# Graph attention on one core: the product q[src] x q[dst] reads q[dst] from PSUM, and the one-hot products are made one block ahead

## The chip, the cores and the metric

The kernel runs on one core of one Trainium2 chip. A core has five engines that run side by side, each with its own queue of instructions: TensorE (PE; its weight loads are listed apart as PEld), VectorE (DVE), ScalarE (ACT), GpSimd (POOL) and SyncE (SP). They wait for each other on semaphores. TensorE writes its results to PSUM, of which there are eight banks; everything else lies in SBUF or in DRAM and is moved by DMA. POOL issues the indirect DMAs (gathers by index), SP all the others of the main loop.

The metric is the time of one execution in microseconds on the device. Nine executions of the kernel before took 3247.66 to 3299.46 us, with a median of 3289.91 us.

## The reference

One layer of a graph network with 12500 nodes and 212500 edges, sorted by dst. All features have 128 elements, 8 heads of 16.

```
h = relu(layernorm(x))
q, v = h @ Wq.T + bq, h @ Wv.T + bv          # per node
k = edge_attr @ Wk.T + bk                    # per edge
in_m   = sum(q[src] * k,      per head)      # three logits per edge and head
out_m  = sum(q[dst] * k,      per head)
diag_m = sum(q[src] * q[dst], per head)
score = (softmax of each, over the edges of one dst; summed) * edge_weight ** lam
h2 = segment_sum(score * v[dst], dst)
out = x + leaky_relu(h2 @ Wo.T + bo, 0.1)
```

The segment softmax has a maximum, an exponential and two sums over the edges of each node. As the edges are sorted, all of these are scans along the edges.

## The kernel before

The path for sorted edges (`ordered_path`) has three parts. A preparation computes q for all nodes and writes it to DRAM twice: `q_table`, in float32, and `q3_table`, as three bfloat16 terms whose sum is q. The main loop goes over the edges. A last part adds up per node and applies Wo.

The main loop works on blocks of 512 edges (128 partitions x JN = 4). The edges are cut into S = 5 stretches, and a step t takes one block of each stretch, s = 0 to 4: T = 84 steps, 420 blocks, and block number g = 5 t + s. For one block:

- `gather` (L608): POOL issues four indirect DMAs, which fetch q[src] from `q_table` into half 0 of the tile qq. It is called LOOK = 9 blocks ahead; there are QQ = 11 qq tiles. A gather waits until the last reader of its tile is done.
- `fetch_edges` (L600): SP loads the edge features ea, 6 blocks ahead into 7 tiles.
- `turn` (L940, L942): TensorE transposes ea into eT_ps, ScalarE copies it to eT.
- `project` (L948, L950): TensorE makes k in k_ps (two banks), the bias first.
- `spread_q` (L959, L961): because edges are sorted by dst, the q[dst] of a block lie within a window of 42 nodes. SP has loaded this window of `q3_table` (the tile win, L926, two tiles with five loads for each step t). Four matmuls of a one-hot matrix (oh) with win put q[dst] into qd_ps, for which there is one bank. ScalarE copies it into half 1 of qq.
- `one_hots` (L934, L935): ScalarE makes the one-hots of the next step from a list of relative indices (relb, loaded by SP, L916).
- `logits` (L968, L969, L971): VectorE multiplies half 0 and half 1 of qq (L968), both halves by k (L969), and sums over 16 elements for each head (L971).

Once per step t, and each at a given s, the scans follow: `turn_logits` and `turn_sums` at s = 0 (L984, L991, L1049, L1050), `scan_max` at s = 1 (L1001, L1004), `to_rows` (the matmuls of w_ps, L1062, and the copy L1067) and `powers` (L1012 to L1019) at s = 2, `scan_sums` (L1025, L1029) and the fetches for step t + 2 (L916, L920, L926) at s = 3, `select` (L1038) and `put_rows` (SP writes the sums, L1074) at s = 4.

The order of the work is written out by hand. `pin` ties each instruction to the one that was pinned before it on the same engine, so each engine, SP's and POOL's queues among them, runs its instructions in the order in which the loop calls them. The loop calls, for each g: gather, fetch_edges, project(g + 1), turn(g + 2), spread_q(g + 2), logits(g), one_hots, and then what s asks for. Where a tile is used again, the waits follow from its last readers.

PSUM is full: two banks each of eT_ps and k_ps, one of qd_ps, three that the small tiles of the scans share.

Of the kernel before, what the change touches and what calls it, by code (L numbers as in the profile page):

```python
# [472 lines left out]
def ordered_path(ctx: ExitStack, tc: tile.TileContext, flag, x, src, dst, edge_attr, edge_weight,  # L473
# [17 lines left out]
    nc = tc.nc  # L491
# [83 lines left out]
    def pin(inst):  # L575

        engine = str(inst.ins.engine)
        if engine in pinned:
            tc.add_manual_dep(inst.ins, pinned[engine], mybir.DependencyInfo(
                mybir.DependencyClass.NoSync, mybir.DependencyReason.DATA), reason="in order")  # L580
        pinned[engine] = inst.ins.name
        return inst
# [8 lines left out]
    qqs, st, eas = {}, {}, {}  # L591

    def fetch_edges(g):
        if g < S * T:
            ea = load.tile([P, JN * F], F32, name="ea", bufs=EA)
            b0 = (g % S * G + g // S) * BE
            n = min(BE, E - b0)
            if n < BE:
                nc.vector.memset(ea, 0.0)
            pin(nc.sync.dma_start(ea[:n // JN, :],  # L600
                                  edge_attr[b0:b0 + n, :].rearrange("(p j) f -> p (j f)", j=JN)))
            eas[g] = ea

    def gather(g):
        if g < S * T:
            qq = gath.tile([P, JN, 2, F], F32, name="qq")
            for j in range(JN):
                pin(nc.gpsimd.indirect_dma_start(  # L608
                    out=qq[:, j, 0, :], out_offset=None, in_=q_table,
                    in_offset=bass.IndirectOffsetOnAxis(  # L610
                        ap=src_i[:, g % S * G + g // S, j:j + 1], axis=0)))
            qqs[g] = qq
# [287 lines left out]
    with tc.tile_pool(name="work", bufs=2) as work, \  # L900
            tc.tile_pool(name="scan", bufs=2) as scan, \
            tc.tile_pool(name="ps", bufs=1, space=PSUM) as ps:
        ks, eTs, lTs, base_v = {}, {}, {}, {}
        end = S * T

        def block_rows(t):
# [3 lines left out]
        def fetch(t):  # L910

            if t >= T:
                return
            at, part = block_rows(t)
            relb = load.tile([K3, S, BE], BF, name="relb")
            pin(nc.sync.dma_start(relb, rel_d[part].rearrange("(s b) e -> s b e", b=G)  # L916
                                  [None, :, at, :].to_broadcast([K3, S, BE])))
            fa = load.tile([4 * S, BE], BF, name="fa", bufs=4)
            for s in range(S):
                pin(nc.sync.dma_start(fa[4 * s:4 * s + 4], fa_d[s * G + t]))  # L920
            _, base_v[t] = nc.values_load_multi_w_load_instructions(
                bases[0:1, t, 0:S], engines=[mybir.EngineType.SP], min_val=0, max_val=N - 1,
                skip_runtime_bounds_check_because="the indices of nodes are below N")
            win = load.tile([K3, S, F], BF, name="win")
            for s in range(S):
                pin(nc.sync.dma_start(win[:, s, :], q3_table[bass.ds(base_v[t][s] * 3, K3), :]))  # L926
            st[t] = dict(relb=relb, fa=fa, win=win)

        def one_hots(t, s):

            if s == 0:
                st[t]["oh"] = work.tile([K3, S, BE], BF, name="oh")
            d = st[t]["relb"][:, s, :]
            pin(nc.scalar.activation(d, d, AF.Abs, bias=before[:K3]))  # L934
            pin(nc.scalar.activation(st[t]["oh"][:, s, :], d, AF.Relu, bias=1.0, scale=-1.0))  # L935

        def turn(g):
            eT_ps = ps.tile([P, JN, P], F32, name="eT_ps", bufs=2)
            for j in range(JN):
                pin(nc.tensor.transpose(eT_ps[:, j, :], eas[g][:, j * F:(j + 1) * F], ident))  # L940
            eT = work.tile([P, JN, P], F32, name="eT", bufs=3)
            pin(nc.scalar.copy(eT, eT_ps))  # L942
            eTs[g] = eT
            del eas[g]

        def project(g):
            k_ps = ps.tile([P, JN, F], F32, name="k_ps", bufs=2)
            pin(nc.tensor.matmul(k_ps, ones3, bk3, start=True, stop=False))  # L948
            for j in range(JN):
                pin(nc.tensor.matmul(k_ps[:, j, :], eTs[g][:, j, :], wk, start=False,  # L950
                                     stop=(j == JN - 1)))
            ks[g] = k_ps
            del eTs[g]

        def spread_q(g):
            s, d = g % S, st[g // S]
            qd_ps = ps.tile([P, JN, F], F32, name="qd_ps")
            for j in range(JN):
                pin(nc.tensor.matmul(qd_ps[:, j, :], d["oh"][:, s, j * P:(j + 1) * P],  # L959
                                     d["win"][:, s, :], start=(j == 0), stop=(j == JN - 1)))  # L960
            pin(nc.scalar.copy(qqs[g][:, :, 1, :], qd_ps))  # L961

        def logits(g):
            s, t = g % S, g // S
            if s == 0:
                lTs[t] = scan.tile([P, JN, S, H3], F32, name="lT")
            prod = work.tile([P, JN, 3, F], F32, name="prod")
            pin(nc.vector.tensor_mul(prod[:, :, 2, :], qqs[g][:, :, 0, :], qqs[g][:, :, 1, :]))  # L968
            pin(nc.vector.tensor_mul(prod[:, :, 0:2, :], qqs[g],  # L969
                                     ks[g][:, :, None, :].to_broadcast([P, JN, 2, F])))  # L970
            pin(nc.vector.tensor_reduce(lTs[t][:, :, s, :],  # L971
                                        prod.rearrange("p j i (h d) -> p j (i h) d", d=DIM), AX.X,
                                        ALU.add))
            del ks[g], qqs[g]

        last = {}

# [100 lines left out]
        def later(f, t):  # L1078
            if 0 <= t < T:
                f(t)  # L1080
# [5 lines left out]
        turn(0)  # L1086
        turn(1)
        spread_q(0)
        spread_q(1)
        project(0)  # L1090
        for g in range(end + 2 * S):
            s, t = g % S, g // S
            if g < end:
                gather(g + LOOK)
                fetch_edges(g + AHEAD)
            if g + 1 < end:
                project(g + 1)
            if g + 2 < end:
                turn(g + 2)
                spread_q(g + 2)  # L1100
            if g < end:
                logits(g)
            if t + 1 < T:
                one_hots(t + 1, s)
            if s == 0:
                later(turn_logits, t - 1)
                later(turn_sums, t - 2)
            elif s == 1:
                later(scan_max, t - 1)
            elif s == 2:  # L1110
                later(to_rows, t - 2)
                later(powers, t - 1)
            elif s == 3:
                later(scan_sums, t - 1)
                if t + 2 < T:
                    fetch(t + 2)
            else:
                later(select, t - 1)
                later(put_rows, t - 2)
# [67 lines left out]
@with_exitstack  # L1187
def kernel(ctx: ExitStack, tc: tile.TileContext, x, src, dst, edge_attr,
                              edge_weight, Wq, bq, Wk, bk, Wv, bv, Wo, bo, lam, out):

    nc = tc.nc
    given = (x, src, dst, edge_attr, edge_weight, Wq, bq, Wk, bk, Wv, bv, Wo, bo, lam, out)
    flags = ctx.enter_context(tc.tile_pool(name="flags", bufs=1))
    flag = flags.tile([1, 1], I32, name="flag")
    ordered_path(tc, flag, *given)
    other = nc.values_load(flag[0:1, 0:1], min_val=0, max_val=1)
    with tc.If(other != 0):
        general_path(tc, *given)  # L1200
# [29 lines left out]
```

## Time and profile before

| | |
|---|---|
| nine executions | 3247.66 to 3299.46 us, median 3289.91 |
| the profiled execution | 3280.52 us, of which the span of its instructions is 3278.7 us |
| granted TensorE clock, mean | 0.727 |
| busy: PE, PEld | 1787.5 us (55%), 1440.6 us (44%) |
| busy: DVE, ACT, POOL | 2140.5 us (65%), 1521.7 us (46%), 1739.4 us (53%) |
| DMA | 345.21 MB, mean 105 GB/s |
| L608, gathers | 1680, 1706.4 us busy, mean 1016 ns, median 947 ns |
| L968, L969, L971 | 420 each, mean 680, 1215, 1753 ns |
| L959, L961 | 1680 with a mean of 261 ns, 420 with a mean of 590 ns |

No engine is busy for more than two thirds of the span. A line of the profile names the line of the kernel, the engine, the operation, what it writes and reads, and shapes; behind them stand the number of instructions, their busy time and the mean of one in ns, and then the idle time of the engine just before them with what ended most of it. "remote" means that a semaphore rose without an instruction in the trace that it can be put down to; "issue" means that the engine waited for nothing that the profile shows. In a timeline the first column is the start in us from the start of the span and the second the time in us; "x5" behind a line means that it stands for five instructions of the same kind, of which the first starts there. The ends of matmuls are modelled.

### The profile page before, as it was taken

The page shows a single profiled execution, that of the slowest core. Times are in us where ns is not written, and L with a number is a line of the kernel's source. Part 1 is how long each engine was busy: PE and PEld are TensorE (multiplying, and loading weights), DVE is VectorE, ACT ScalarE, POOL GpSimd, SP SyncE. Part 2 cuts the span into 40 slices and gives each one's busy share as a digit, 9 for nine tenths or more (in the row PEclk, how much of TensorE's full clock was granted, in tenths as well). Part 3 has the DMA queues.
Part 4 walks back from the last instruction along what each step waited for, and adds up shares of the span by engine and source line. Part 5 has one row for each costly group of instructions (what it writes and reads, how often), then busy time and mean ns, then how long its engine had stood idle before and what let it go on. Part 6 is the DMA issues. An engine that isn't in the chain of part 4 may idle for free. (4 is left out here: it accounts for less than half of the span.)

```text
span 3278.7 us, 35097 instructions
## 1 busy us (share of the span) xinstructions
PE 1787.5 (55%) x10635; PEld 1440.6 (44%) x10635; DVE 2140.5 (65%) x2178; ACT 1521.7 (46%) x2806; POOL 1739.4 (53%) x1714
## 2 busy tenths in 40 slices
PE   5245555555556545555545456555555546556567
PEld 4134444444444444444444344444444444445445
DVE  6556757667666667666667667566667666667754
ACT  5444445445454444444445444444445445445445
POOL 3545656646655556645656656555656555656100
PEclk8556767767776777777777767767767767767779
DMA  6643333333333333333333333333333333333152
GB/s 199 222 135 96 103 94 114 101 95 106 99 100 100 93 100 107 100 88 109 97 94 113 96 100 105 97 92 106 97 93 114 93 100 105 95 95 113 26 139 80
DMA packets 307123, 345.21 MB, mean 105 GB/s; under 512 B 134531, under 2 KB 225944, under 8 KB 306613
## 3 DMA queue, kind: packets, MB, share of 16 engines
q1 hardware_dynamic: 252474, 229.91, 23.6%
q0 software_dynamic: 54448, 112.96, 12.4%
q8 instruction: 85, 1.39, 0.2%
q14 instruction: 116, 0.95, 0.1%
HBM read 309.91 MB, written 32.76 MB: 105 GB/s over the span
## 5 line engine op out<-in xcount | busy, mean ns | idle before, releaser
L608 POOL DMA_INDIRECT qq<-q_table,src_i x1680 | 1706.4, 1016 | 1242.4 <-ACT qq L961 567.2
L950 PE MATMUL k_ps<-wk,eT 128*128 128x128 f32 x3360 | 658.0, 356 | 990.9 <-ACT eT L942 939.4
L950 PEld LDWEIGHTS k_ps<-wk,eT 128*128 128x128 f32 x3360 | 557.4, 251 | 1227.6 <-ACT eT L942 1044.3
L971 DVE TENSOR_REDUCE lT<-prod 128x96 f32<-128x1536 f32 x420 | 736.2, 1753 | 14.3
L1025 DVE TENSOR_TENSOR ew<-e,att_ps 120x512 f32<-120x512 f32 x84 | 57.8, 688 | 923.8 <-ACT e L1016 715.7
L942 ACT COPY eT<-eT_ps 128x512 f32<-128x512 f32 x420 | 246.2, 586 | 619.1 <-PE eT_ps L940 252.7
L969 DVE TENSOR_TENSOR prod<-qq,k_ps 128x1024 f32<-128x1024 f32 x420 | 510.4, 1215 | 26.7 <-remote 19.2
L1067 ACT COPY rows<-w_ps 126x288 f32<-126x288 f32 x84 | 33.6, 400 | 822.1 <-remote 783.9
L940 PE MATMUL eT_ps<-ident,ea 128*128 128x128 f32 x1680 | 344.2, 343 | 3.0 <-DVE found L881 2.9
L934 ACT ACTIVATE relb<-relb,before 126x512 bf16<-126x512 bf16 x420 | 307.7, 733 | 6.9 <-DMA relb<-rel_d 6.9
L968 DVE TENSOR_TENSOR prod<-qq 128x512 f32<-128x512 f32 x420 | 285.8, 680 | 15.1 <-ACT qq L961 10.4
L961 ACT COPY qq<-qd_ps 128x512 f32<-128x512 f32 x420 | 247.8, 590 | 81.6 <-remote 23.0
L959 PE MATMUL qd_ps<-win,oh 126*128 126x128 bf16 x1680 | 220.5, 261 | 117.4 <-issue 76.8
L940 PEld LDWEIGHTS eT_ps<-ident,ea 128*128 128x128 f32 x1680 | 277.0, 183 | 3.6 <-DVE found L881 3.2
L935 ACT ACTIVATE oh<-relb 126x512 bf16<-126x512 bf16 x420 | 265.3, 632 | 13.4
L948 PE MATMUL k_ps<-b,ones 3*128 3x512 bf16 x420 | 189.3, 451 | 102.8 <-issue 62.5
L959 PEld LDWEIGHTS <-oh 126*128 126x128 bf16 x1680 | 170.8, 121 | 119.8 <-issue 73.6
L1049 PE MATMUL b_ps<-ident,sum 120*128 120x120 f32 x672 | 127.0, 314 | 128.5 <-ACT l L991 123.0
L1062 PE MATMUL w_ps<-back,sel 128*126 128x144 f32 x1344 | 186.9, 293 | 1.3 <-ACT back L1050 1.3
L1062 PEld LDWEIGHTS w_ps<-back,sel 128*126 128x126 f32 x1344 | 172.9, 192 | 2.0 <-ACT back L1050 2.0
L1049 PEld LDWEIGHTS b_ps<-ident,sum 120*128 120x128 f32 x672 | 95.2, 212 | 166.4 <-ACT l L991 137.6
L1050 ACT COPY back<-b_ps 128x480 f32<-128x480 f32 x168 | 97.7, 582 | 40.2 <-PE b_ps L1049 38.9
(155 smaller groups left out, 1746.3 us busy)
## 6 DMA issues: line engine op xcount, KB each, us to landing
ea<-in_edge_attr_dram SPq DMA_DIRECT2D x419, 256.0 KB
relb<-rel_d SPq DMA_DIRECT2D x84, 630.0 KB
qq<-q_table,src_i POOLq DMA_INDIRECT x1680
win<-q_table SPq DMA_DIRECT2D x420, 31.5 KB
q_table<-q SPq DMA_DIRECT2D x24, 384.0 KB
fa<-fa_d SPq DMA_DIRECT2D x420, 4.0 KB
sums<-rows SPq DMA_DIRECT2D x416, 7.9 KB
q_table<-xq SPq DMA_DIRECT2D x24, 256.0 KB
```

What stands on the lines that cost most here:

```text
L608: pin(nc.gpsimd.indirect_dma_start(out=qq[:, j, 0, :], out_offset=None, in_=q_table, in_offset=bass.IndirectOffsetOnAxis(ap=src_i[:, g % S ...
L934: pin(nc.scalar.activation(d, d, AF.Abs, bias=before[:K3]))
L935: pin(nc.scalar.activation(st[t]["oh"][:, s, :], d, AF.Relu, bias=1.0, scale=-1.0))
L940: pin(nc.tensor.transpose(eT_ps[:, j, :], eas[g][:, j * F:(j + 1) * F], ident))
L942: pin(nc.scalar.copy(eT, eT_ps))
L950: pin(nc.tensor.matmul(k_ps[:, j, :], eTs[g][:, j, :], wk, start=False, stop=(j == JN - 1)))
L959: pin(nc.tensor.matmul(qd_ps[:, j, :], d["oh"][:, s, j * P:(j + 1) * P], d["win"][:, s, :], start=(j == 0), stop=(j == JN - 1)))
L961: pin(nc.scalar.copy(qqs[g][:, :, 1, :], qd_ps))
L968: pin(nc.vector.tensor_mul(prod[:, :, 2, :], qqs[g][:, :, 0, :], qqs[g][:, :, 1, :]))
L969: pin(nc.vector.tensor_mul(prod[:, :, 0:2, :], qqs[g], ks[g][:, :, None, :].to_broadcast([P, JN, 2, F])))
L971: pin(nc.vector.tensor_reduce(lTs[t][:, :, s, :], prod.rearrange("p j i (h d) -> p j (i h) d", d=DIM), AX.X, ALU.add))
L1062: pin(nc.tensor.matmul(w_ps[:, i].rearrange("p s c -> p (s c)"), d["sel"][:, j, lo:lo + 3, :].rearrange("p s w -> p (s w)"), d["back"][:, ...
```

## The change

L968 reads q[dst] from qd_ps instead of from half 1 of qq. The copy into half 1 remains, because L969 multiplies both halves by k. As qd_ps has one bank, the one-hot products of a block can't be made before L968 of the block before has read it; `spread_q` is called for g + 1 instead of g + 2, between project(g + 1) and turn(g + 2). Before the loop it is called for block 0 alone.

```diff
             pin(nc.scalar.copy(qqs[g][:, :, 1, :], qd_ps))
+            qds[g] = qd_ps

         def logits(g):
...
             prod = work.tile([P, JN, 3, F], F32, name="prod")
-            pin(nc.vector.tensor_mul(prod[:, :, 2, :], qqs[g][:, :, 0, :], qqs[g][:, :, 1, :]))
+            pin(nc.vector.tensor_mul(prod[:, :, 2, :], qqs[g][:, :, 0, :], qds[g]))
...
-            del ks[g], qqs[g]
+            del ks[g], qds[g], qqs[g]
...
         spread_q(0)
-        spread_q(1)
         project(0)
         for g in range(end + 2 * S):
...
             if g + 1 < end:
                 project(g + 1)
+                spread_q(g + 1)
             if g + 2 < end:
                 turn(g + 2)
-                spread_q(g + 2)
             if g < end:
                 logits(g)
```

In the order of the built program TensorE's first matmul of L959 waits for VectorE where it waited for ScalarE, and L968 waits for ScalarE's copy L961 of the same block. On SP and POOL the instructions stand in the same order as before; the first of SP's five win loads of a step waits, as before, for the last one-hot product that read the tile. From L962 on, lines of the changed kernel have numbers that are higher by one.

More of the change, by code (lines that the diff above doesn't have):

```diff
@@ L902, in ordered_path @@
             tc.tile_pool(name="ps", bufs=1, space=PSUM) as ps:
-        ks, eTs, lTs, base_v = {}, {}, {}, {}
+        ks, eTs, qds, lTs, base_v = {}, {}, {}, {}, {}
         end = S * T
```

## The prediction

> **What bounds the kernel now.** I read the page's costliest groups first, then the waits, then one stretch of the timeline, and last the windows. A round below is the five blocks (s = 0 to 4) of one step t: 20 gathers by POOL (L608), five products on VectorE, one pass of the scans. The groups show a busy POOL and two long waits:
>
> ```profile
> L608 POOL DMA_INDIRECT qq<-q_table,src_i x1680 | 1706.4, 1016 | 1242.4 <-ACT qq L961 567.2
> ...
> L1025 DVE TENSOR_TENSOR ew<-e,att_ps 120x512 f32<-120x512 f32 x84 | 57.8, 688 | 923.8 <-ACT e L1016 715.7
> ...
> L1067 ACT COPY rows<-w_ps 126x288 f32<-126x288 f32 x84 | 33.6, 400 | 822.1 <-remote 783.9
> ```
>
> VectorE idles 923.8 us before L1025, which needs ScalarE's e, and ScalarE idles 822.1 us just before it, at L1067, for the matmuls of w_ps. The timeline of one round (start, us, engine) shows how they hang together:
>
> ```profile
> 1700.21 0.69 DVE L968 TENSOR_TENSOR prod<-qq 128x512 f32<-128x512 f32 x1
> ...
> 1700.34 1.37 POOL L608 DMA_INDIRECT qq<-q_table,src_i  x1 [0.30 <-issue]
> 1700.38 2.18 PE L1062 MATMUL w_ps<-back,sel 128*126 128x144 f32 x16
> ...
> 1702.50 4.95 SPq L926 DMA_DIRECT2D win<-q_table  x5
> 1702.51 0.59 ACT L961 COPY qq<-qd_ps 128x512 f32<-128x512 f32 x1 [0.86 <-remote]
> ...
> 1714.54 0.95 POOL L608 DMA_INDIRECT qq<-q_table,src_i  x1 [0.30 <-issue]
> 1715.26 0.40 ACT L1067 COPY rows<-w_ps 126x288 f32<-126x288 f32 x1 [10.88 <-remote]
> ...
> 1717.26 0.69 DVE L1025 TENSOR_TENSOR ew<-e,att_ps 120x512 f32<-120x512 f32 x1 [9.93 <-ACT down L1013]
> ...
> 1720.81 1.22 DVE L969 TENSOR_TENSOR prod<-qq,k_ps 128x1024 f32<-128x1024 f32 x1
> ...
> 1722.77 0.95 POOL L608 DMA_INDIRECT qq<-q_table,src_i  x1 [7.28 <-ACT eT L942]
> ...
> 1723.73 1.02 DVE L1038 TENSOR_TENSOR sel<-ends,places 128x840 f32<-128x840 f32 x1
> ...
> 1724.02 1.56 POOL L608 DMA_INDIRECT qq<-q_table,src_i  x1 [0.30 <-DVE lT L971]
> ```
>
> The rows of w_ps end at 1702.56, yet ScalarE's copy is let go at 1715.26, at the end of POOL's burst of 20 gathers (the last runs from 1714.54 to 1715.49; in the round before, the burst ended at 1679.22 and the copy came at 1681.85). Then ScalarE's four powers, L1025, two scans and L968 and L969 follow, and 0.74 us after L969 ends (1722.03) a buffer is free and the next burst starts. So a round is **burst plus rest**: 26.1 us (1689.35 to 1715.49) plus a rest of 7.3 us (here) or 10.1 us (the round before, 1679.22 to 1689.35; 36.3 in all). What holds TensorE's releases back the trace doesn't name; that the gathers belong to it the windows show (length; busy us of PE, PEld, DVE, ACT, POOL):
>
> ```profile
> 1690.00:1726.00 36.00, 20.53 (x134) 16.66 (x132) 25.87 (x25) 17.94 (x33) 22.32 (x23) 0.76 0.35 102
> ...
> 3070.00:3092.00 22.00, 16.60 (x113) 13.76 (x112) 21.83 (x21) 11.66 (x22) 0.00 (x0) 0.84 0.01 3
> ```
>
> Once the gathers are done, VectorE is busy 21.83 of 22 us, and the copies L1067 come 22.8 and 20.5 us apart (3069.08, 3091.86, 3112.36). With gathers it is busy 25.87 of 36.
>
> **The change, part by part.** Against the profiled execution (3280.5 us, 9 us under the median 3289.9 of the nine times).
>
> 1. L968 reads q[dst] from PSUM. Its length stays: L969 has one PSUM operand and takes 1215 ns for 1024 elements against 680 for 512 with both in SBUF, 1.04 ns per further element, so a start cost of about 0.15 us in both; L1025 (one PSUM operand, 688 ns) and L1004 (none, 692) agree. 420 x 0.00 us; bounds from these rows ±0.01, ±4 us.
>
> What it does to POOL: a bare gather takes 947 ns (median of L608), the mean is 1016, so 1680 x 69 ns = 116 us are spent held up. In every burst three gathers are long: 1.57, 1.31 and 1.37 us at 1690.60, 1694.97 and 1700.34. The last two begin under an L968 (1694.78 and 1700.21, 0.68 each), the first under L1038; gathers under L969 and L971 take 0.95. L968 and L1038 read two SBUF operands, L969 one. The gather of 1700.34 ends 0.81 us after L968 does, a bare one lasts 0.95, so it needs what L968 has 0.14 us after its own start. With q[dst] in PSUM the two holds go: 0.36 + 0.42 = 0.78 us a round. L1038's hold (0.62) stays. Next late is L1004, also two SBUF operands, 1699.60 to 1700.29: the gather that followed it at 1700.34 will start 0.37 sooner, at 1699.97, need its input at 1700.11 and wait 0.2. So 0.6 us a round remain, in some 82 rounds with gathers 48 us; bounds 0.28 (L1004 holds 0.5) and 0.78: 23 to 64 us. As burst and rest stand end to end, I let all of it reach the span.
>
> The Trainium skill has a rule against this gain: in "SBUF — State Buffer", "Who interferes with whom", a tensor_tensor with two SBUF inputs contends with GpSimd's reads of SBUF, but was not seen to stall DMA issue, because descriptors are said (inferred) to need the write side. By that the gain would be zero; the rows of 1.31 and 1.37 us beside 0.95 say otherwise, and I go by them.
>
> 2. The one-hot products (L959, 1680 matmuls) and ScalarE's copy L961 (420 x 0.59) stay in number. They move from behind the transposes of g + 2 to ahead of them, one block later, and the matmuls wait for L968 of the block before (one buffer, qd_ps); L968 in turn waits for the copy. Behind the waiting matmul stand eT of g + 2 and, in s = 2, w_ps; behind the copy ScalarE's eT copy and the one-hots. The chain from the end of L968 to the next: matmuls 0.39 to 0.63, copy 0.59, hand-overs some 0.2, together 1.3. On VectorE L969 and L971 lie between, 2.83 us (1700.90 to 1703.73). So 1.5 us of cover a block where releases are prompt: cost 0.
>
> 3. w_ps now stands behind the products of s = 3, which wait for L968 of s = 2 (end 1700.90), then L940: it starts near 1702.0 instead of 1700.4. If its release counted from its own start that costs 1.6 us a round, 131 us; if from the end of the burst, 0. The nearest rows (copy 12.7 us after the end of w_ps, but 2.6 us after the last gather or during it) say 0; I keep 131 for the range.
>
> 4. SP's five win loads (L926) reuse the buffer that the products of s = 4 read last, now issued a block later, behind w_ps. SP leaves the held stretch. What is queued behind them, an ea load and the sums, is used a round or several blocks later: cost 0. The gain is unknown: between 0 and the 5.0 to 7.0 us (1702.50 and 1669.84) that these issues take inside it. I take 0, as the burst's end explains both rounds.
>
> 5. Before the loop one block's products less: under 1.3 us, once.
>
> Sum: 48 us of 3280.5, 1.5%; on the median 3290 - 48 = **3242 us**.
>
> **Rivals.**
> *A larger gain.* TensorE's releases and SP's issues are slow in the same stretch (five win issues 5.0 and 7.0 us, five sums issues outside it 4.1 and 3.0), so they may share what is slow. Without SP there, w_ps is released earlier by up to 5 us a round; a rest of 7.3 to 10.1 has room for that. 82 x 5.0 = 410, so 2830 at the far end; half of it, 3037. Against: releases come right behind the burst's end. Chance 0.20.
>
> *No change.* The gain in POOL goes into a longer rest, since the rest ends on VectorE (L1025 to L969), or L1004 and L1038 hold the gathers that slide under them. 3257 to 3323. Chance 0.20.
>
> *Slower: a second rest.* In the held stretch a release of the products comes late: the copies of s = 4 start 1.96 us (1700.55 to 1702.51) and in the round before 5.4 us (1664.42 to 1669.85) after their matmuls' rows end. Today nothing waits for them; afterwards L968 of s = 3 does. Cover: 1.5 us on VectorE, plus POOL's: the block's buffer is free at 1706.28 and needed at 1710.79, 0.8 sooner afterwards, so 3.7; together 5.2 us. Beyond it, POOL stops after 16 gathers, VectorE finishes s = 3 only then, and if w_ps is let go only after the last four gathers the round has a rest more. Its length: 2.6 to the release, copy 0.6, L968 0.7, L969 1.2 and 0.7 until POOL starts, 5.8 us. 82 x 5.8 = 476 in every round, or 3718 us; in one of three 159, or 3401 us. It decides from a late release of 5.2 us, which one of the two rounds above has. Chance 0.30.
>
> **The numbers.** Forecast 0.30, larger gain 0.20, no change 0.20, second rest 0.30. About 1% is what nine times of this kernel (3248 to 3299) can tell from none. The forecast's own span, 3226 to 3267 by part 1's bounds, lies partly within 1% (0.05): faster 0.45, same 0.25, slower 0.30. The range reaches to the half of the larger gain, to a second rest in one round of three, and so over part 3's end (3242 + 131 = 3373): 3040 to 3400, with some 0.1 left out on either side.
>
> **What would show it.** Right: L608's mean falls from 1016 to about 980 ns, the long gathers under L968 are gone and one of 1.56 a round stays; bursts near 25.5 us; rests still 7 to 10; L968 nearly without idle time. Larger gain: L1067's 822 us fall well below 600 and L1025's with them. Second rest: two gaps over 2 us between gathers per round, idle time before L968 on ScalarE's L961. I am wrong if rests change by more than bursts do, since I hold them constant without knowing what holds TensorE's releases.

## The result and the profile after

The changed kernel takes 3092.9 us (median of 15 runs, 3082.0 to 3104.2), the kernel before 3275.1 us in all its 46 runs beside it: ratio 0.945, 95% interval 0.943 to 0.947. That is 182 us less; the forecast had 48 us less.

In two jobs the kernel before took 3275 and 3386 us and in the four others 2477 to 2481 us (one chip was seen both ways), while all runs of a job agree, so each kernel is compared with the kernel before of its own job; jobs of the first kind are called late and those of the second prompt, after what their traces show of TensorE's releases (the moment at which a semaphore lets the engine go on that waits for a matmul).

The profiled execution after takes 3094.5 us (span 3092.6). These are the costliest groups of its page that answer to those shown of before; the columns are busy us and mean ns, then the idle time just before and what ended most of it:

```profile
L608 POOL DMA_INDIRECT qq<-q_table,src_i x1680 | 1656.3, 986 | 1118.5 <-issue 504.0
...
L961 ACT COPY qq<-qd_ps 128x512 f32<-128x512 f32 x420 | 246.3, 586 | 1078.2 <-remote 553.5
L969 DVE TENSOR_TENSOR prod<-qq,qd_ps 128x512 f32<-128x512 f32 x420 | 286.3, 682 | 695.5 <-ACT qq L961 469.7
...
L1026 DVE TENSOR_TENSOR ew<-e,att_ps 120x512 f32<-120x512 f32 x84 | 57.8, 688 | 73.1 <-ACT e L1017 40.4
```

The list of all groups adds the line of the rows' copy, with its releasers one by one:

```profile
L1068 ACT COPY rows<-w_ps 126x288 f32<-126x288 f32 x84 | 32.8, 391 | 53.1 <-PE w_ps L1063 26.9 <-remote 14.7 <-issue 10.9
```

POOL's gathers are 50.1 us less busy (1706.4 to 1656.3) and 123.9 us less idle (1242.4 to 1118.5). The other 12 us of the span's 186 lie outside: the first gather starts 7.5 us sooner, and from the start of the last one to the end it takes 4.6 us less. The long waits of before are nearly gone: 822 to 53 us ahead of the rows' copy, 924 to 73 us ahead of the product ew. In their place VectorE waits 695.5 us at L969, mostly for ScalarE's copy L961, and ScalarE 1078.2 us at L961, 553.5 of it for a release that the trace can't put down to an instruction and 189.3 for the matmuls of qd_ps. A round in the timeline of the changed kernel (start, us, engine; in brackets the idle time before):

```profile
1702.10 0.95 POOL L608 DMA_INDIRECT qq<-q_table,src_i  x1 [3.77 <-ACT oh L935]
...
1703.57 2.43 PE L1063 MATMUL w_ps<-back,sel 128*126 128x144 f32 x16
...
1706.04 0.40 ACT L1068 COPY rows<-w_ps 126x288 f32<-126x288 f32 x1 [0.35 <-issue]
...
1711.26 2.96 SPq L926 DMA_DIRECT2D win<-q_table  x5
1711.27 0.59 ACT L961 COPY qq<-qd_ps 128x512 f32<-128x512 f32 x1 [2.77 <-remote]
...
1714.44 0.95 POOL L608 DMA_INDIRECT qq<-q_table,src_i  x1 [2.64 <-ACT eT L942]
...
1725.76 0.63 PE L959 MATMUL qd_ps<-win,oh 126*128 126x128 bf16 x4
...
1728.82 0.94 POOL L608 DMA_INDIRECT qq<-q_table,src_i  x1 [0.30 <-issue]
1731.77 0.59 ACT L961 COPY qq<-qd_ps 128x512 f32<-128x512 f32 x1 [5.84 <-remote]
...
1732.39 0.69 DVE L969 TENSOR_TENSOR prod<-qq,qd_ps 128x512 f32<-128x512 f32 x1 [6.15 <-ACT qq L961]
...
1732.99 1.22 DVE L970 TENSOR_TENSOR prod<-qq,k_ps 128x1024 f32<-128x1024 f32 x1
...
1734.95 0.95 POOL L608 DMA_INDIRECT qq<-q_table,src_i  x1 [5.18 <-ACT oh L935]
```

POOL goes on at 1702.10, 1714.44 and 1734.95, each time after a pause of 2.6 to 5.2 us; before it had one pause in a round. The w_ps matmuls start 1.47 us after a restart and end at 1706.00; their copy follows at 1706.04. The products of L959 that start at 1725.76 end at 1726.39, but the copy is let go at 1731.77, 2.0 us after the last gather. From that copy to the next gather it is 3.18 us (L961, L969, L970), where it was 7.5 us from the rows' copy (1715.26 to 1722.77).

Over gathers 60 to 1620 the kernel before has 80 pauses of more than 1 us, of 8.72 us in the mean, 76 of them after exactly 20 gathers; the changed one has 171 of 3.47 us, most of them after 4, 8, 12 or 16 gathers. Together that is 698 and 593 us.

How late a release is can be counted: the time from the end of the matmuls to the start of ScalarE's copy that waits for them (L942, L961 and the rows' copy), for all copies ahead of which ScalarE stood idle, sorted by how long POOL had then been gathering without such a pause. Medians in us:

| gathering for | before | after | order only, late job | changed kernel, prompt job |
|---|---|---|---|---|
| under 5 us, or POOL standing still | 0.04 | 0.04 | 0.04 | - |
| 5 to 10 us | 0.04 | 2.50 | 0.04 | - |
| 10 to 12 us | 1.28 | 2.43 | 3.34 | - |
| 12 to 15 us | 8.91 | 4.32 | 4.69 | - |
| over 15 us | 13.45 | 5.39 | 13.47 | 0.04 |

In a late job releases are late, in the median, only when gathers have run for several us, and most of those over 5 us late come during the last gathers or within 3 us of the last one's end. In a prompt job POOL gathers for 2000 us without a pause, and the releases take 0.04 us. So lateness isn't a trait of the program alone; what it is, neither the traces nor the runs name.

One rival can be ruled out from the traces. The mean granted clock of TensorE was lower in the late jobs (0.69 to 0.73) than in the prompt ones (0.79 to 0.82; 0.755 for the changed kernel). But in the changed kernel's prompt run 265 of these copies fell at a granted clock below 0.6 (mean over the 2 us behind the matmuls, or up to the copy where that is longer), and none waited over 0.04 us. In its late run 133 fell at over 0.9, and half of them waited more than 1 us. So a low clock alone doesn't make releases late; whether lateness lowers the mean clock isn't shown.

### The profile page after: what moved, and what is told of

Its sections match the earlier page's. It is cut to its first block, busy times and chain, and to the rows that moved or that the text cites. A ratio compares the mean times of both kernels' runs of the same rounds, so it can differ in the third digit from the quotient of the medians.

```text
span 3092.6 us, 35097 instructions
## 1 busy us (share of the span) xinstructions
PE 2058.5 (67%) x10635; PEld 1641.5 (53%) x10635; DVE 2159.3 (70%) x2178; ACT 1538.4 (50%) x2806; POOL 1689.3 (55%) x1714
## 4 chain that ended last, share of the span: by engine, by line
PE 33%; another core or an unknown queue 20%; ACT 20%; issue 13%; DVE 8%; DMA 3%; SPq 1%; POOL 1%; ACTq 0%; DVEq 0%; POOLq 0%
PE k_ps L950 13%; PE eT_ps L940 6%; ACT eT L942 4%; PE w_ps L1063 4%; ACT qq L961 3%; PE qd_ps L959 3%; ACT relb L934 3%; PE b_ps L1050 2%; DVE prod L970 2%; DMA qq<-q_table,src_i 2%; PE k_ps L948 1%; DVE sum L1030 1%; DVE prod L969 1%; ACT l L992 1%
## 5 line engine op out<-in xcount | busy, mean ns | idle before, releaser
L608 POOL DMA_INDIRECT qq<-q_table,src_i x1680 | 1656.3, 986 | 1118.5 <-issue 504.0
L950 PE MATMUL k_ps<-wk,eT 128*128 128x128 f32 x3360 | 755.9, 395 | 723.4 <-ACT eT L942 448.8
L950 PEld LDWEIGHTS k_ps<-wk,eT 128*128 128x128 f32 x3360 | 643.2, 286 | 895.6 <-ACT eT L942 526.3
L961 ACT COPY qq<-qd_ps 128x512 f32<-128x512 f32 x420 | 246.3, 586 | 1078.2 <-remote 553.5
L969 DVE TENSOR_TENSOR prod<-qq,qd_ps 128x512 f32<-128x512 f32 x420 | 286.3, 682 | 695.5 <-ACT qq L961 469.7
L970 DVE TENSOR_TENSOR prod<-qq,k_ps 128x1024 f32<-128x1024 f32 x420 | 510.4, 1215 | 0.5 <-PE k_ps L950 0.5
L940 PE MATMUL eT_ps<-ident,ea 128*128 128x128 f32 x1680 | 403.0, 388 | 2.9 <-DVE found L881 2.9
L942 ACT COPY eT<-eT_ps 128x512 f32<-128x512 f32 x420 | 246.7, 588 | 170.0 <-remote 115.8
L959 PE MATMUL qd_ps<-win,oh 126*128 126x128 bf16 x1680 | 240.4, 291 | 72.8 <-ACT oh L935 30.6
L959 PEld LDWEIGHTS <-oh 126*128 126x128 bf16 x1680 | 193.0, 137 | 111.7 <-issue 64.2
L1063 PE MATMUL w_ps<-back,sel 128*126 128x144 f32 x1344 | 237.6, 345 | 1.3 <-ACT back L1051 1.3
L1063 PEld LDWEIGHTS w_ps<-back,sel 128*126 128x126 f32 x1344 | 235.4, 250 | 2.0 <-ACT back L1051 2.0
L1002 DVE TENSOR_TENSOR_SCAN u<-l,u,far_ps 120x512 f32<-120x512 f32 x83 | 105.5, 1271 | 3.1 <-ACT l L992 3.0
```

Of the source, the lines that this page charges most:

```text
L608: pin(nc.gpsimd.indirect_dma_start(out=qq[:, j, 0, :], out_offset=None, in_=q_table, in_offset=bass.IndirectOffsetOnAxis(ap=src_i[:, g % S ...
L970: pin(nc.vector.tensor_mul(prod[:, :, 0:2, :], qqs[g], ks[g][:, :, None, :].to_broadcast([P, JN, 2, F])))
L1063: pin(nc.tensor.matmul(w_ps[:, i].rearrange("p s c -> p (s c)"), d["sel"][:, j, lo:lo + 3, :].rearrange("p s w -> p (s w)"), d["back"][:, ...
```

## The experiments

The experiments began with three theories. Theory A: the place of the products shortens the rests, the PSUM operand adds the 50 us of POOL. Theory B: the operand does it all. Theory S, the rival that the prediction called a larger gain: SP's win loads in the late stretch hold up TensorE's releases.

### The order alone

```diff
-            pin(nc.vector.tensor_mul(prod[:, :, 2, :], qqs[g][:, :, 0, :], qds[g]))
+            pin(nc.vector.tensor_mul(prod[:, :, 2, :], qqs[g][:, :, 0, :], qqs[g][:, :, 1, :]))
```

(on the changed kernel). Run twice, first in a prompt job:

> The changed kernel, but L969 reads both halves of qq from SBUF again, so only the order is changed: spread_q(g + 1) ahead of turn(g + 2), one block ahead. Theory A (what shortens the rests is the new place of the one-hot products, and with them that of SP's win loads): the holds of the gathers come back, some 50 us, the rest of the gain stays; 3093 + 50 = 3143, ratio to the kernel before 0.96. Theory B (the PSUM operand does it all, by freeing the gathers of holds): 3275, ratio 1.00. By both, long gathers of 1.3 us under L969 are there again, L608's mean near 1016 ns.

Measured: 2478.3 us beside 2479.5, ratio 1.001 (0.999 to 1.002). No release is late and POOL never pauses, so there are no rests to shorten:

```profile
L608 POOL DMA_INDIRECT qq<-q_table,src_i x1680 | 1658.6, 987 | 545.0 <-issue 427.4
```

L608's mean is 987 ns, not the 1016 expected, but that of the kernel before in such a job is 989 (with three win tiles, below), so the order frees no gather; its idle time of 545 us is little more than the 0.30 us ahead of each of 1680 gathers (504 us). In a late job:

> The order of the changed kernel with L969 reading half 1 of qq from SBUF, as in the first run of it. Where the kernel before takes 2480 us: ratio 1.00 again. Where it takes about 3275: theory A (the new place of the products shortens the rests) 3143, ratio 0.96; theory B (the PSUM operand does it all) 3275, ratio 1.00.

Measured: 3348.0 us beside 3386.1, ratio 0.988 (0.986 to 0.989): neither A (0.96) nor B (1.00). The page, and then one round of the timeline:

```profile
L608 POOL DMA_INDIRECT qq<-q_table,src_i x1680 | 1708.6, 1017 | 1320.0 <-ACT eT L942 751.0
...
L1026 DVE TENSOR_TENSOR ew<-e,att_ps 120x512 f32<-120x512 f32 x84 | 57.8, 688 | 863.6 <-ACT e L1017 802.5
...
L1068 ACT COPY rows<-w_ps 126x288 f32<-126x288 f32 x84 | 33.5, 399 | 763.8 <-remote 753.4
```

```profile
1663.85 2.12 PE L1063 MATMUL w_ps<-back,sel 128*126 128x144 f32 x16
...
1669.27 2.08 PE L950 MATMUL k_ps<-wk,eT 128*128 128x128 f32 x8 [2.72 <-issue]
...
1676.24 0.94 POOL L608 DMA_INDIRECT qq<-q_table,src_i  x1 [0.30 <-issue]
1679.97 0.40 ACT L1068 COPY rows<-w_ps 126x288 f32<-126x288 f32 x1 [9.48 <-remote]
1680.16 2.46 SPq L926 DMA_DIRECT2D win<-q_table  x5
...
1687.48 0.95 POOL L608 DMA_INDIRECT qq<-q_table,src_i  x1 [10.30 <-ACT eT L942]
```

The gathers are held as before (mean 1017) and the long wait is back at the rows' copy. The w_ps matmuls end at 1665.97, 14 us ahead of their copy; POOL's last gather ends at 1677.18, 2.79 us ahead of it; and 7.5 us after the copy starts POOL goes on. The ends of matmuls are modelled, but TensorE had gone on to the next matmuls of k_ps at 1669.27: what is late is the release. **S falls by this**: the win loads (L926) go out here at 1680.16, right behind that copy (and at 1643.75 in the round before). They have left the late stretch, and w_ps is released as late as before (a median of 13.8 us after its end; 13.9 in the profile of the kernel before). In 79 of the 84 rounds the copy comes more than 5 us late, and in none of them does SP issue any DMA between the end of the matmuls and the copy. Without SP's loads in it, the stretch is the same.

### The PSUM operand alone

```diff
-            pin(nc.vector.tensor_mul(prod[:, :, 2, :], qqs[g][:, :, 0, :], qqs[g][:, :, 1, :]))
+            pin(nc.vector.tensor_mul(prod[:, :, 2, :], qqs[g][:, :, 0, :], ks[g]))
```

(on the kernel before; q[dst] is left out of the third logit). Prompt, then late:

> The kernel before in its own order, but L968 multiplies q[src] by k_ps in PSUM instead of by q[dst]; this leaves q[dst] out of the third logit, so the output isn't the reference's, while the instructions stay the same in number and size. It prices the holds alone. Theory A: 48 us less than before (3275 - 48 = 3227, ratio 0.985), rests unchanged, L1067's idle time still near 800. Theory B: near the changed kernel's 3093, ratio 0.945. By both: no gather over 1.2 us under L968, L608's mean near 985.

Measured: 2456.6 us beside 2479.5, ratio 0.991 (0.989 to 0.993), and L608 falls by 29 us against the order alone:

```profile
L608 POOL DMA_INDIRECT qq<-q_table,src_i x1680 | 1629.2, 970 | 547.3 <-issue 446.0
```

> The kernel before in its own order with L968 multiplying q[src] by k_ps from PSUM (q[dst] left out of the third logit), as in the first run of it. Where the kernel before takes 2480 us: ratio 0.991 again. Where it takes about 3275: theory A 3227, ratio 0.985; theory B 3093, ratio 0.945.

Measured: 3282.2 us beside 3386.1, ratio 0.970 (0.968 to 0.971); A said 0.985, B 0.945.

```profile
L608 POOL DMA_INDIRECT qq<-q_table,src_i x1680 | 1658.8, 987 | 1294.6 <-ACT qq L961 576.4
...
L942 ACT COPY eT<-eT_ps 128x512 f32<-128x512 f32 x420 | 245.8, 585 | 1091.1 <-remote 613.2
...
L968 DVE TENSOR_TENSOR prod<-qq,k_ps 128x512 f32<-128x512 f32 x420 | 284.5, 677 | 360.7 <-remote 298.2
...
L1025 DVE TENSOR_TENSOR ew<-e,att_ps 120x512 f32<-120x512 f32 x84 | 57.8, 688 | 602.1 <-ACT e L1016 593.8
```

The list of all groups has for the rows' copy:

```profile
L1067 ACT COPY rows<-w_ps 126x288 f32<-126x288 f32 x84 | 32.8, 390 | 100.3 <-remote 60.0 <-PE qd_ps L959 30.8 <-PE w_ps L1062 9.5
```

POOL is busy 49.8 us less than with the order alone in the same job, as forecast, and idle 25.4 us less. The whole gain on the kernel before is 104 us, more than twice what the holds are worth; as the kernel before left no profile in this job, how the 104 us divide isn't measured, but pauses must be in it. Over gathers 60 to 1620 there are 109: 47 still follow 20 gathers, but 29 follow 16 and 29 follow 4, where VectorE waited at L968 for the release of k_ps (which this L968 needs; without the edit L969, right behind it, does). ScalarE's wait has moved from the rows' copy (100.3 us) to the eT copy ahead of it in its queue (L942, 1091.1 us). So freeing gathers also moves the point of the round at which POOL first runs out of buffers. I had taken that point as fixed.

### Both together again

The changed kernel, in a late and in a prompt job:

> The changed kernel itself once more. In the four runs before this one the kernel before took 2480 us and not 3275, and no release of TensorE was late there. Where that is so again: the order costs and brings nothing and the PSUM operand brings the holds of the gathers, 20 to 25 us, ratio 0.991. Where the kernel before takes about 3275 us: ratio 0.945 as at first.

Measured: 3158.2 us beside 3386.1, ratio 0.933 (0.931 to 0.936); 0.945 was expected.

```profile
L608 POOL DMA_INDIRECT qq<-q_table,src_i x1680 | 1657.3, 986 | 1176.7 <-issue 474.8
...
L969 DVE TENSOR_TENSOR prod<-qq,qd_ps 128x512 f32<-128x512 f32 x420 | 286.8, 683 | 725.4 <-ACT qq L961 495.0
```

In this job the order alone brought 38 us, the operand alone 104 and both 228, 86 us more than the sum, where the interval of each is 6 to 8 us to either side. The 182 us of the first late job, in which the kernel before took 3275 us, weren't divided in this way. Against the order alone (spans 3355.3 and 3159.3) POOL is busy 51 us less and idle 143 us less; against the operand alone (3278.5) 1.5 us and 118 us less. So the order, with the tie of TensorE to VectorE that only the kernel with both edits has, is worth 118 us of POOL's pauses where the gathers are free, and the order is worth 38 us in all where they are held. The w_ps matmuls start here, in the median, 1.4 us after a restart of POOL (12.6 us with the order alone) and their copy follows 0.2 us after their end (13.8 us).

> The changed kernel once more, beside the three that follow. Where the kernel before takes 2480 us, POOL issues gathers without a pause and sets the time (its gathers lead by 1.5 blocks), so only the freed gathers count: 1680 x 0.012 to 0.017 us, ratio 0.988 to 0.991. Where it takes over 3200 us: 0.933 to 0.945 again.

Measured: 2443.8 us beside 2480.1, ratio 0.987 (0.984 to 0.989), 36 us less; 0.988 to 0.991 was expected.

```profile
L608 POOL DMA_INDIRECT qq<-q_table,src_i x1680 | 1622.3, 966 | 542.4 <-issue 420.6
...
L969 DVE TENSOR_TENSOR prod<-qq,qd_ps 128x512 f32<-128x512 f32 x420 | 284.4, 677 | 105.4 <-DMA qq<-q_table,src_i 65.2
```

POOL's gathers are 36 us less busy than with the order alone (1658.6), as much as the whole gain; L969 waits mostly for a gather's landing. Time held, counted as what gathers of more than 1 us take above 947 ns from 200 us on, is 30 us here and 66 us with the order alone.

### Three win tiles

```diff
-            win = load.tile([K3, S, F], BF, name="win")
+            win = work.tile([K3, S, F], BF, name="win", bufs=3)
```

(on the kernel before; SP's win loads no longer wait for the products of the step before). Four times, all in prompt jobs:

> The kernel before, but three win tiles instead of two (in the pool work, where there is room): SP's five win loads no longer wait for the products of s = 4 and go out right behind the fa loads, near the burst's beginning, and not in the stretch in which the release of w_ps is late. Theory S (SP's issues and TensorE's releases share what is slow, so each win issue in that stretch costs w_ps about 0.7 us): w_ps is released up to 5 us earlier, rests 3 to 5 us shorter, 3275 - 130 or more, ratio 0.96 or less; L1067's idle time falls by 100 to 400 us. Theory A or B: 3275, ratio 1.00.

> The kernel before with three win tiles, so that SP's win loads go out before TensorE's releases become late, as in the first run of it. Where the kernel before takes over 3200 us: theory S (SP's issues share what is slow with TensorE's releases): 0.96 or less, the idle time of L1067 falls by 100 us or more. Without S: 1.00. Where it takes 2480 us: 1.00 again.

> The kernel before with three win tiles, as in the first run of it. Where the kernel before takes over 3200 us: theory S (SP's issues share what is slow with TensorE's releases) 0.96 or less, the idle time of L1067 falls by 100 us or more; without S 1.00. Where it takes 2480 us: 1.00 again.

> The kernel before with three win tiles. Where the kernel before takes over 3200 us: theory S (SP's issues share what is slow with TensorE's releases) 0.96 or less, the idle time of L1067 falls by 100 us or more; without S 1.00. Where it takes 2480 us: 1.00 again.

Measured: ratios 1.001, 1.000, 1.000 and 1.002 (1.000 to 1.003). As no release was late in these jobs, the runs say of S only that the loads cost nothing there. What they give is the kernel before with prompt releases, since it differs from it in SP's queue alone:

```profile
L608 POOL DMA_INDIRECT qq<-q_table,src_i x1680 | 1661.1, 989 | 544.2 <-issue 433.4
...
L968 DVE TENSOR_TENSOR prod<-qq 128x512 f32<-128x512 f32 x420 | 286.7, 683 | 164.8 <-DMA qq<-q_table,src_i 128.4
```

L968 waits for the gathers' landing (128 us), POOL for nothing. S rests on the order alone in the late job.

### The transposes first

```diff
                 project(g + 1)
-                spread_q(g + 1)
             if g + 2 < end:
                 turn(g + 2)
+            if g + 1 < end:
+                spread_q(g + 1)
```

(on the changed kernel). Three times, all prompt:

> The changed kernel, but spread_q(g + 1) is called behind turn(g + 2) instead of ahead of it, so the products are still made one block ahead and still wait for VectorE's product of the block before, but don't hold up the transposes of g + 2. If the place ahead of the transposes is what shortens the rests, the time goes back by most of 130 us (ratio over 0.97). If it is that the products are made one block ahead, or the win loads that follow them, it stays at 3093, ratio 0.945, or falls, as k_ps no longer waits for eT (723 us of idle time of L950 before the matmuls).

> The changed kernel with spread_q(g + 1) behind turn(g + 2), as in the first run of it. Where the kernel before takes over 3200 us: if the place ahead of the transposes matters, over 0.95; if one block ahead is all that matters, 0.933 to 0.945. Where it takes 2480 us: 0.990 again.

> The changed kernel with spread_q(g + 1) behind turn(g + 2). Where the kernel before takes over 3200 us: over 0.95 if the place ahead of the transposes matters, 0.933 to 0.945 if one block ahead is all. Where it takes 2480 us: 0.990 again.

Measured: ratios 0.990, 0.990 and 0.993 (2457, 2458 and 2459 us), 13 to 15 us more than the changed kernel in its prompt job. The gathers are busy 1637 to 1642 us instead of 1622: more of them are held by the two products that still hold any (127 in the first run from 200 us on, 89 in the changed kernel). Whether the place ahead of the transposes matters with late releases wasn't seen.

### The order without the tie, and two banks

The changed kernel ties TensorE to VectorE: the products of a block wait for L969 of the block before. The first kernel takes the tie away (q[dst] left out of the third logit), the second loosens it by a block, with the complete product:

```diff
-            pin(nc.vector.tensor_mul(prod[:, :, 2, :], qqs[g][:, :, 0, :], qds[g]))
+            pin(nc.vector.tensor_mul(prod[:, :, 2, :], qqs[g][:, :, 0, :], ks[g]))
```

```diff
-            eT_ps = ps.tile([P, JN, P], F32, name="eT_ps", bufs=2)
+            eT_ps = ps.tile([P, JN, P], F32, name="eT_ps", bufs=1)
...
-            qd_ps = ps.tile([P, JN, F], F32, name="qd_ps")
+            qd_ps = ps.tile([P, JN, F], F32, name="qd_ps", bufs=2)
```

> The changed kernel with its order, but L969 multiplies q[src] by k_ps (PSUM) instead of by qd_ps, so q[dst] is left out of the third logit: the gathers have no hold under L969 and the order is the changed one, but TensorE's products no longer wait for VectorE's product of the block before, and L969 no longer waits for ScalarE's copy. In the last three runs the order alone brought 1.2%, the PSUM operand alone 3.1%, both together 6.7% (kernel before 3386 us). Theory T (what both together bring beyond the sum, some 2.4%, is the tie of TensorE to VectorE through the one bank): ratio about 0.957. Theory H (order and free gathers work together without the tie): 0.933 or lower. Where the kernel before takes 2480 us: 0.991 by both.

> The order of the changed kernel with L969 reading k_ps (q[dst] left out of the third logit), as in the first run of it. Where the kernel before takes over 3200 us: theory T 0.957, theory H 0.933 to 0.945, level with the changed kernel. Where it takes 2480 us: 0.985 again.

> The order of the changed kernel with L969 reading k_ps (q[dst] left out of the third logit), so that the gathers are free and TensorE isn't tied to VectorE by the bank of qd_ps. Where the kernel before takes over 3200 us: theory T (the tie brings what is beyond the sum) about 0.957, theory H (order and free gathers suffice) 0.933 to 0.945. Where it takes 2480 us: 0.987 again.

> The changed kernel with two banks for qd_ps and one for eT_ps instead of one and two: the product of q[src] and q[dst] is complete, the products of a block wait for L969 of two blocks before and not of one, and the transposes of a block wait for ScalarE's copy of the block before. Theory T (the tie to VectorE helps): slower than the changed kernel by up to 2.4%. Theory H: as the changed kernel or faster, 0.93 to 0.94. Where the kernel before takes 2480 us: 0.990, as the changed one with the transposes first.

> The changed kernel with two banks for qd_ps and one for eT_ps, as in the first run of it. Where the kernel before takes 2480 us: 0.988 again, level with the changed kernel within 0.3%. Where it takes over 3200 us: theory T (the tie to VectorE helps) slower than the changed kernel by up to 2.4%; theory H (order and free gathers suffice) level with it or faster.

Measured, all in prompt jobs: untied 0.985 (0.983 to 0.987), 0.989 and 0.988; two banks 0.988 (0.986 to 0.990) and 0.990 (0.989 to 0.992); the changed kernel 0.987 (0.984 to 0.989) in the job of the second of each. The first untied run:

```profile
L608 POOL DMA_INDIRECT qq<-q_table,src_i x1680 | 1628.8, 970 | 542.1 <-issue 440.2
```

All free the gathers of the hold under L969 and are level with the changed kernel within 0.5%, so with prompt releases the tie costs nothing and none of these is a better kernel. With late releases neither ran: whether the 86 us beyond the sum come from the tie or from order and free gathers alone stays open.

## Why the prediction was right and wrong

**The step that failed** is the one from the burst to the span: "As burst and rest stand end to end, I let all of it reach the span", with rests held at 7 to 10 us. POOL's busy time fell by 50.1 us, where 48 (23 to 64) were forecast; POOL's idle time, pauses that were forecast to stay, fell by 123.9 us. The prediction named this as what would make it wrong ("if rests change by more than bursts do"). I had read the rest as what follows a burst of 20 gathers. It is what follows the late release that VectorE needs first, and both its place in the round and its length go by which release that is. What makes the releases late stays open, and so does whether the order or the tie brings the 86 us beyond the sum.

The measured time lies within the stated range of 3040 to 3400 us, but by luck: it is there below the forecast's own span (3226 to 3267) because half of the larger gain was let in, and the reason given for that gain fell.

Part 1, the operand: right in the trace. L969 keeps its length (682 ns against 680), L608's mean falls to 986 (forecast about 980), no gather is held under L969 (276 overlap it and no other product of two SBUF operands, and the longest takes 0.96 us), 79 are under L1039 (L1038 before) with 1.55 us, and 61 under L1005 with 1.16, the next hold that the prediction named. In one round:

```profile
1715.41 1.02 DVE L1039 TENSOR_TENSOR sel<-ends,places 128x840 f32<-128x840 f32 x1
1715.69 1.56 POOL L608 DMA_INDIRECT qq<-q_table,src_i  x1 [0.30 <-issue]
...
1717.21 0.69 DVE L969 TENSOR_TENSOR prod<-qq,qd_ps 128x512 f32<-128x512 f32 x1 [0.77 <-issue]
...
1717.56 0.95 POOL L608 DMA_INDIRECT qq<-q_table,src_i  x1 [0.30 <-issue]
```

With prompt releases 36 us less of held time are 36 us less in the whole. The Trainium skill ("SBUF — State Buffer", "Who interferes with whom") says that a tensor_tensor with two SBUF inputs wasn't seen to stall DMA issue. Here 160 gathers of the kernel before that began under such an L968 took 1.34 us in the mean beside 0.95, and the same product with one input in PSUM holds none, so for indirect gathers the measurement decides against it.

Part 2, the moved products at no cost: right where releases are prompt (in that job L969 idles 105 us, 65 of them for a gather), wrong where they are late. The cover of 1.5 us on VectorE is gone there, and L969 waits for L961 (469.7 us). The prediction had this under its slower rival.

Part 3, w_ps behind the products of s = 3 at no cost: the cost is none, but for another reason. The w_ps matmuls begin later and often just behind a restart of POOL, where a release takes 0.04 us (table above): in 43 of the 84 rounds after, the rows' copy follows their end within 1 us, before in 4. Where the release of qd_ps is the late one, ScalarE waits for it at L961, in front of the rows' copy.

Part 4 and the larger gain: the direction and the place were right (the rows' copy waits 53 us, not 822), the reason was not. The order alone moves the win loads out of the stretch, and w_ps stays as late (13.8 us).

The second rest: its signs came. There are two pauses a round, and L969 waits on L961. But it priced a rest on top of the first, 5.8 us more. In the trace the long one through the four powers and the scans (7.5 us from copy to gather) went, and shorter ones (3.18 us) took its place: 171 x 3.47 us instead of 80 x 8.72.

## What to carry to other kernels

A wait that is put down to "remote" on every round is not a fixed cost: ask which release the next engine needs first, and how long the chain behind it is, before taking the rest of the round as given. Where a change touches both a hold and an order, run each alone beside both, since here 38 and 104 us made 228. And put the kernel before in every job: the same program on the same chip took 2480 us in one and 3386 us in another, and what a change is worth went from 1.3% to 6.7%.

## What the runs showed of the hardware

In the late jobs TensorE's releases come up to 16.9 us late (profile of the kernel before) while POOL issues indirect gathers. They begin to be late 5 to 12 us after POOL begins (table above), and most of those over 5 us late come within 3 us of its last gather's end at the latest. In prompt jobs, with gathers without a pause, the same kernel's releases take 0.04 us. A gather of 128 rows takes 0.95 us, also where it overlaps a VectorE product with one SBUF operand, and 1.16 to 1.56 us in the mean where it is held under one with two. With prompt releases POOL sets the time: 1680 gathers at 0.95 and 0.30 us are 2100 of 2440 us. There, once the tiles that were filled ahead are used up, the gathers issued lead VectorE by 1.5 to 2 blocks; with late releases they lead by 10 of 11.
